# Inverse square roots of the layer norms: a power on GpSimd and one Newton step, instead of a bit trick and three steps on VectorE

## The chip, the core and the metric

The kernel runs on one core of one Trainium2 chip. The metric is the device time of one execution in microseconds (us). The profile names the engines: PE is TensorE's matrix products and PEld its weight loads, DVE is VectorE, ACT is ScalarE, POOL is GpSimd, and SP is SyncE, whose queue issues nearly all DMAs. All engines run on their own, each through its own list of instructions in order, and they wait for one another through semaphores.

## The reference, cut to what matters

One transformer block with adaptive layer norm, on x of 2 batches x 2048 rows x 256 columns:

```
mod = silu(c) @ wmod                      # six rows of 256 for each batch
sa, ca, ga, sb, cb, gb = six parts of mod # |ga|, |gb| raised to at least 0.25
norm(x) = (x - mean(x)) / sqrt(var(x) + 1e-5)      # over the 256 columns

h = norm(x) * (1 + ca) + sa
q, k, v  = projections of h               # 16 heads, keys of 16, values of 64
attn = softmax(q k^T / 4, axis = query)   # normalised over the queries
x = x + ga * (attn v) @ output_proj

h = norm(x) * (1 + cb) + sb
f(a, w) = fp4(a) @ fp4(w)^T               # blocks of 16, scale max/6, 8 levels and a sign
x = x + gb * f(silu(f(h, w_gate)) * f(h, w_up), w_down)     # 704 hidden columns
```

The change concerns the 1 / sqrt(var + 1e-5) in the two norms.

## The kernel before

The work is cut into chains, Python generators that yield one operation (or a group) at a time. A planner (`Order`, L111) picks greedily, by estimated costs, due times and free buffers, which chain goes on next, and so writes out by hand the order of every engine's instructions. The estimates of an operation are in `Queue.estimate` (L287). For a POOL operation on two tensors it takes 0.08 us and 0.0023 us an element (L321), and 0.2 us for a dependence from one engine to another (`CROSS`, L113). All operations are recorded through L273, so the profile tells groups apart by tile names and not by lines. The planner also holds POOL and some forms on DVE apart (`port`).

The attention runs over 2 batches, 16 heads in each and 16 blocks of 128 keys in each head: 512 steps. In a step (`scores` L1031, `step` L1091) PE forms the scores of 128 keys and 2048 queries (`ps`) in two halves. DVE copies each half out of PSUM, negated and scaled, with the running minimum (`e<-ps`, its longest kind of work). POOL merges the two minima (`mn`). ACT takes the exponential with the sum (`z`). DVE forms `rz` = 1/z, POOL scales the values with it (`vn`), and PE adds up the output (`o<-e,vn`) some steps later (LAG, 4.5). Five `e` buffers and three places for scores in PSUM bound how far the engines run ahead of each other.

Beside these steps lie, by their due times:

- the first norm (`norm` L835). Batch 0's four groups of 512 rows are at the very start, before there is any attention to lie beside; batch 1's four groups stand beside the last heads of batch 0. A group's statistics (`ln_stats` L574) are followed by `ln_apply` (L611, tile `xn`, on ACT or DVE as the planner chooses), PE transposes (`ht`), two copies with scale and bias (`ht`, one on ACT, one on DVE), and the q, k and v projections (`qk`, `v`). The copies `st` feed DMAs that bring q and k into the layout for the scores.
- the quantising of the weights (`quantize_exactly` L703, tiles `wg`, `wu`, `wd`, `qx`, `sp`), in batch 0.
- the output projections (`project` L1181, tiles `op`, `x`).
- the feed-forward part of batch 0 (`ffn_stats` L1266, `ffn` L1290), beside the attention of batch 1. It quantises its rows on DVE, ACT and POOL (`quantize` L648).
- after the last step, the tail: the last projections, the second norm (`ffn_stats`, `tail_norm` L1375) and the feed-forward part of batch 1 (`tail` L1404), with no attention left beside it.

At the start ACT also forms the modulation's columns (`sa_t` and `ca_t`, from PE's product `modt`); the modulation's rows (`modb`, `mods`) come from PE and are reworked on DVE. A filler of identity transposes (`busy`) runs on PE before that.

`ln_stats` (L574) is called with up to 4 tiles of 128 rows. For each it runs two statistics instructions (`bst` and `mv`, in the profile `sta`/`mva` or `stf`/`mvf`). Then it works on 128 x 4 values: `ln0` is the variance plus 1e-5, `ln1` the inverse root, `ln2` a scratch, `ln3` the mean times minus the root. Tiles of the first norm end in a, those of the second in f. The inverse root comes from shifting the bits of `ln0` right by one and subtracting them from a constant (L590 to L593), and then three Newton steps, of three operations each in the first two and four in the last (L594 to L600). All of it is on DVE. Each of these tiles has two buffers, and the room `ln` lets two calls be under way at once.

Of the kernel before, what the change touches and what calls it, by code (L numbers as in the profile page):

```python
# [10 lines left out]
F32 = mybir.dt.float32  # L11
F32R = mybir.dt.float32r
I32 = mybir.dt.int32
U32 = mybir.dt.uint32
AF = mybir.ActivationFunctionType
ALU = mybir.AluOpType
# [4 lines left out]
P = 128  # L21
# [313 lines left out]
def adaln_block(  # L335
# [14 lines left out]
    nc = tc.nc  # L350
# [24 lines left out]
    T, V, A, G, S = (  # L375
        Queue(n, e)
        for n, e in (
            ("PE", nc.tensor),
            ("DVE", nc.vector),
            ("ACT", nc.scalar),  # L380
            ("POOL", nc.gpsimd),
            ("SP", nc.sync),
        )
# [11 lines left out]
    const = ctx.enter_context(tc.tile_pool(name="const", bufs=1))  # L395
# [96 lines left out]
    ident = const.tile([P, P], F32, tag="ident", name="ident")  # L492
    make_identity(nc, ident)
    magic = const.tile([P, 2], F32, tag="magic", name="magic")
    nc.gpsimd.memset(magic[:, 0:1], 1.5 * 2.0 ** 22)
    nc.gpsimd.memset(magic[:, 1:2], -1.5 * 2.0 ** 22)

# [76 lines left out]
    def ln_stats(x4, name, centre=False):  # L574


        n = x4.shape[1]
        yield Wait(take=["ln"])
        mv = small.tile([P, 4, 2], F32, tag="mv", name=f"mv{name}", bufs=2)
        for t in range(n):  # L580
            st = small.tile([P, 6], F32, tag="bst", name=f"st{name}_{t}")
            yield Free(V.bn_stats(st, x4[:, t, :]))
            yield V.bn_aggr(mv[:, t, :], st)
        v, r, e, c = (
            small.tile([P, 4], F32, tag=f"ln{i}", name=f"ln{i}{name}", bufs=2)[:, 0:n]
            for i in range(4)
        )
        yield V.tensor_scalar(v, mv[:, 0:n, 1], EPS, None, ALU.add)

        yield V.tensor_scalar(r.bitcast(U32), v.bitcast(U32), 1, None, ALU.logical_shift_right)  # L590
        yield V.tensor_scalar(
            r.bitcast(I32), r.bitcast(I32), -1.0, float(0x5F3759DF), ALU.mult, ALU.add
        )  # L593
        for i in range(3):  # L594
            yield V.tensor_tensor(e, r, r, ALU.mult)
            yield V.scalar_tensor_tensor(e, e, -0.5, v, ALU.mult, ALU.mult)
            if i < 2:
                yield V.scalar_tensor_tensor(r, e, 1.5, r, ALU.add, ALU.mult)
        yield V.scalar_tensor_tensor(e, e, 0.5, r, ALU.add, ALU.mult)
        yield V.tensor_tensor(r, r, e, ALU.add)  # L600
        if centre:
            return mv[:, :, 0], r
        yield V.scalar_tensor_tensor(c, mv[:, 0:n, 0], -1.0, r, ALU.mult, ALU.mult)
        return c, r
# [230 lines left out]
    def norm(b, g):  # L835
# [8 lines left out]
        if b not in h_t:  # L844
            h_t[b] = hp.tile([P, KC, N], F32, tag="ht", name=f"ht{b}")
        c, r = yield from ln_stats(x4, f"a{b}_{g}")
        if b == 0:
            place, _ = yield Wait(["sa"], ["s", "e"])
# [417 lines left out]
    def ffn_stats(b, t, n):  # L1266
        yield Wait([("out", b, NQUAD - 1, t + j) for j in range(n)])
        x4 = xs[b, t // 4][:, t % 4 : t % 4 + n, :]
        c, r = yield from ln_stats(x4, f"f{b}_{t}", centre=b == B - 1)
        for j in range(n):  # L1270
            lns[b, t + j] = (c, r, j, n)
        signal(("ln", b, t))
# [361 lines left out]
```

## Time and profile before

| what | value |
|---|---|
| median of 3 runs | 1929.37 us (1929.2 to 1930.44) |
| the profiled execution's own time | 1929.38 us |
| its span, first to last instruction | 1927.6 us |
| granted TensorE clock | 1.00 |
| DVE, 128 x 4 `ln2a<-ln1a` product | 24 times, 152 ns each |
| POOL, 128 x 1 `mn<-mn` | 512 times, 298 ns each |
| POOL, 128 x 64 `vn<-v,rz` | 512 times, 323 ns each |
| first scores on PE (`ps<-q,k`) | at 42.38 us |
| last attention output on PE before the tail's first projection | until 1749.3 us |

A line of the timeline or of a group names the engine, the operation, the tile written and the tiles read (`out<-in`), and the shape. A timeline line begins with the start in us from the span's start and the duration; in brackets at its end is the idle time of the engine just before it, and what ended that. A group's line ends with the busy time, the mean of one in ns, and the idle time of the engine just before these instructions. The chain of waits is followed back from the last instruction: at each step to what released it, or to the instruction before it on its engine.

### The profile page before, as it was taken

How to read it: one execution, taken by the hardware profiler on the slowest of the kernel's cores; microseconds unless marked ns; L12 is line 12 of the kernel's file. 1: busy time of each engine (PE TensorE's matmuls, PEld its weight loads, DVE VectorE, ACT ScalarE, POOL GpSimd, SP SyncE). 2: the span in 40 equal slices, each digit the busy share in tenths (PEclk: the TensorE clock that was granted, in tenths of full speed). 3: DMA queues.
4: the chain of work that ended last, by engine and by line, in shares of the span. 5: the costliest groups of instructions: out<-in, count | busy, mean ns of one | idle time of the engine just before them, and what ended most of it. 6: DMA issues, size and time to landing. Idle time of an engine off the chain costs nothing.

```text
span 1927.6 us, 30282 instructions
## 1 busy us (share of the span) xinstructions
PE 1898.0 (98%) x10212; PEld 787.2 (41%) x10212; DVE 1711.0 (89%) x4170; ACT 1317.7 (68%) x1428; POOL 617.2 (32%) x1387
## 2 busy tenths in 40 slices
PE   9999999999999999999999999999999999999998
PEld 5333433343334333343334434334434343335666
DVE  5999999999999998888888788887888888997997
ACT  4787677777776676777777667676676777884333
POOL 0333333333443331113444344444443211230010
PEclk9999999999999999999999999999999999999999
DMA  6422121202120223211102210211011111100000
GB/s 211 100 67 55 38 56 50 47 19 49 46 62 4 50 55 94 77 39 45 52 16 61 64 44 18 55 36 39 9 37 44 34 34 34 39 1 1 12 17 17
DMA packets 40395, 88.02 MB, mean 46 GB/s; under 512 B 6320, under 2 KB 22576, under 8 KB 36272
## 3 DMA queue, kind: packets, MB, share of 16 engines
q1 hardware_dynamic: 38880, 83.98, 16.9%
q8 instruction: 82, 1.34, 0.3%
q10 hardware_dynamic: 1360, 2.10, 0.3%
q14 instruction: 73, 0.60, 0.1%
HBM read 63.51 MB, written 20.97 MB: 44 GB/s over the span
## 4 chain that ended last, share of the span: by engine, by line
PE 84%; DVE 13%; ACT 2%; issue 1%; POOL 0%; ACTq 0%; POOLq 0%; DVEq 0%
PE o L273 43%; PE ps L273 15%; DVE e L273 8%; PE op L273 6%; PE v L273 6%; PE dn L273 3%; PE qk L273 2%; PE up L273 2%; PE gate L273 2%; PE h2t L273 1%; DVE w L273 1%; PE pg L273 1%; PE pu L273 1%; ACT e L273 1%; PE busy L273 1%
## 5 line engine op out<-in xcount | busy, mean ns | idle before, releaser
L273 DVE TENSOR_SCALAR_CACHE_REDUCE e<-ps 128x1024 f32<-128x1024 f32 x1024 | 1226.1, 1215 | 90.5 <-PE ps L273 65.6
L273 ACT ACTIVATE e<-e,mn 128x2048 f32<-128x2048 f32 x512 | 1025.2, 2002 | 393.1 <-POOL mn L273 391.3
L273 PE MATMUL o<-e,vn 128*64 128x512 f32 x4096 | 993.4, 603 | 5.9 <-ACT osb L273 2.2
L273 PEld LDWEIGHTS o<-e,vn 128*64 128x64 f32 x4096 | 255.0, 136 | 454.1 <-issue 371.4
L273 POOL TENSOR_SCALAR mn<-mn 128x1 f32<-128x1 f32 x512 | 152.3, 298 | 731.4 <-DVE rz L273 285.3
L273 PE MATMUL ps<-q,k 64*128 64x512 f32 x2048 | 371.4, 445 | 2.2 <-DVE e L273 1.7
L273 PEld LDWEIGHTS ps<-q,k 64*128 64x128 f32 x2048 | 159.7, 184 | 346.6 <-DVE e L273 116.4
L273 POOL TENSOR_SCALAR vn<-v,rz 128x64 f32<-128x64 f32 x512 | 165.5, 323 | 309.2 <-DVE rz L273 217.4
L273 PE MATMUL op<-wo,osb 128*64 128x256 f32 (+1 forms) x960 | 125.3, 382 | 2.5 <-DVE x L273 1.8
L273 PE MATMUL v<-wv,ht 128*64 128x256 f32 x1024 | 124.0, 381 | 0.9 <-DVE st L273 0.6
L273 DVE RECIPROCAL rz<-z 128x1 f32<-128x1 f32 x512 | 80.3, 157 | 26.5 <-ACT e L273 25.5
L273 PEld LDWEIGHTS op<-wo,osb 128*64 128x64 f32 (+1 forms) x960 | 74.3, 140 | 61.1 <-issue 22.6
L273 PEld LDWEIGHTS v<-wv,ht 128*64 128x64 f32 x1024 | 71.3, 137 | 65.0 <-issue 26.9
L273 ACT ACTIVATION_READ_ACCUMULATOR e<-e,mn 128x1 f32 x512 | 95.4, 186 | 0.0
L273 DVE DVE_READ_ACCUMULATOR e<-ps 128x1 f32 x1024 | 84.2, 82 | 0.0
L273 ACT COPY osb<-o 64x512 f32<-64x512 f32 x104 | 60.2, 579 | 23.6 <-PE o L273 21.7
L273 PE MATMUL qk<-ht,wqk_sb 128*64 128x512 f32 (+1 forms) x224 | 61.7, 598 | 0.9 <-ACT ht L273 0.9
L273 POOL TENSOR_TENSOR h<-h,m 128x704 f32<-128x704 f32 x32 | 54.1, 1689 | 12.6 <-DVE m L273 7.9
L273 DVE TENSOR_TENSOR x<-op,x 128x512 f32<-128x512 f32 (+1 forms) x61 | 41.2, 676 | 13.7 <-PE op L273 13.3
L273 PE MATMUL dn<-wdb,e 117*128 117x256 f32 (+1 forms) x192 | 45.1, 382 | 3.3 <-ACT e L273 3.1
L273 ACT ACT_TABLE_LOAD x34 | 43.6, 1283 | 4.3 <-issue 3.7
L273 PE MATMUL dn<-wd_t,h2t 117*64 117x256 f32 (+1 forms) x384 | 45.8, 381 | 0.0
(243 smaller groups left out, 1454.8 us busy)
## 6 DMA issues: line engine op xcount, KB each, us to landing
k<-scr SPq DMA_DIRECT2D x124, 256.0 KB, 4.6
scr<-st SPq DMA_DIRECT2D x32, 512.0 KB, 3.2
q<-scr SPq DMA_DIRECT2D x124, 128.0 KB, 5.6
x<-in_x_dram SPq DMA_DIRECT2D x8, 512.0 KB, 4.4
wv<-in_wv_dram SPq DMA_DIRECT2D x8, 256.0 KB, 3.7
wo<-in_wo_dram SPq DMA_DIRECT2D x8, 256.0 KB, 2.7
xt<-in_x_dram SPq DMA_DIRECT2D x4, 512.0 KB, 7.2
out_dram<-h2t SPq DMA_DIRECT2D x16, 128.0 KB, 1.8
```

Of the source, the lines that this page charges most:

```text
L273: op = Op(self.name, *self.estimate(method, args, kw, lambda: f(*args, **kw)))
```

## The change

`ln_stats` takes the inverse root from one instruction on POOL, which raises `ln0` to the power of -0.5 (a tensor of exponents, `half_root`, is set once at the start), and keeps one Newton step of four operations on DVE. The bit trick and two Newton steps are gone. The planner's estimates are unchanged, so POOL's new instruction is planned as any product of two tensors of 4 elements.

```diff
     magic = const.tile([P, 2], F32, tag="magic", name="magic")
+    half_root = const.tile([P, 4], F32, tag="half_root", name="half_root")
+    nc.gpsimd.memset(half_root, -0.5)
     nc.gpsimd.memset(magic[:, 0:1], 1.5 * 2.0 ** 22)
...
         yield V.tensor_scalar(v, mv[:, 0:n, 1], EPS, None, ALU.add)
 
-        yield V.tensor_scalar(r.bitcast(U32), v.bitcast(U32), 1, None, ALU.logical_shift_right)
-        yield V.tensor_scalar(
-            r.bitcast(I32), r.bitcast(I32), -1.0, float(0x5F3759DF), ALU.mult, ALU.add
-        )
-        for i in range(3):
-            yield V.tensor_tensor(e, r, r, ALU.mult)
-            yield V.scalar_tensor_tensor(e, e, -0.5, v, ALU.mult, ALU.mult)
-            if i < 2:
-                yield V.scalar_tensor_tensor(r, e, 1.5, r, ALU.add, ALU.mult)
+        yield G.tensor_tensor(r, v, half_root[:, 0 : r.shape[1]], ALU.pow)
+        yield V.tensor_tensor(e, r, r, ALU.mult)
+        yield V.scalar_tensor_tensor(e, e, -0.5, v, ALU.mult, ALU.mult)
         yield V.scalar_tensor_tensor(e, e, 0.5, r, ALU.add, ALU.mult)
         yield V.tensor_tensor(r, r, e, ALU.add)
```

In the code `v`, `r` and `e` are the tiles `ln0`, `ln1` and `ln2`; `V` is DVE and `G` is POOL.

## The prediction

> **What bounds the kernel now.** I read the page's busy times and slices first, then the stretches (busy time of each engine in chosen windows), then the timeline of the first 45 us, and last the chain of waits of the tail.
>
> ```profile
> PE 1898.0 (98%) x10212; PEld 787.2 (41%) x10212; DVE 1711.0 (89%) x4170; ACT 1317.7 (68%) x1428; POOL 617.2 (32%) x1387
> ```
>
> TensorE (PE) idles 29.6 us of 1927.6. VectorE (DVE) has 89% and could bind where its share is higher. So I ask stage by stage.
>
> ```profile
> 15.00:42.40 27.40, 24.90 (x103) 11.56 (x101) 15.74 (x66) 14.35 (x25) 0.00 (x0) 1.00 0.60 175
> 640.00:720.00 80.00, 76.78 (x408) 27.93 (x405) 79.41 (x239) 57.27 (x62) 24.72 (x58) 1.00 0.16 40
> 900.00:1500.00 600.00, 598.99 (x3474) 240.89 (x3472) 506.80 (x1222) 420.53 (x445) 266.13 (x481) 1.00 0.16 40
> 1800.00:1880.00 80.00, 74.41 (x321) 54.14 (x320) 77.29 (x222) 28.11 (x47) 6.26 (x5) 1.00 0.04 15
> ```
>
> The columns are the stretch, its length, and PE, PEld, DVE, ACT and POOL busy with instruction counts. From 900 to 1500, where the feed-forward part of batch 0 lies beside attention, PE is full (598.99 of 600) and DVE has 15% to spare: there a shorter DVE stream buys nothing. From 640 to 720, where batch 1 is normalised, DVE is full (79.41 of 80) and PE is not. The tail is alike: the chain of waits from 1774 to 1880 runs mostly over DVE.
>
> ```profile
> by line: DVE e L273 32.3%; DVE w L273 17.1%; DVE am_g L273 8.0%; PE pg L273 6.9%; PE pu L273 5.9%; DVE r_g L273 3.7%; issue 3.1%; PE dn L273 2.7%; DVE am_h L273 2.6%; POOL w L273 2.3%; DVE q_g L273 1.9%; DVE stf L273 1.8%; ACT e L273 1.8%;
> ```
>
> At the start the timeline decides:
>
> ```profile
> 16.85 0.81 DVE L273 TENSOR_SCALAR ht<-ht,ca_t,sa_t 128x512 f32<-128x512 f32 x1 [3.59 <-ACT ht L273]
> ...
> 17.58 0.15 DVE L273 SCALAR_TENSOR_TENSOR ln1a<-ln2a,ln1a 128x4 f32<-128x4 f32 x1
> ...
> 19.19 0.14 DVE L273 SCALAR_TENSOR_TENSOR ln3a<-mva,ln1a 128x4 f32<-128x4 f32 x1
> ...
> 19.37 2.08 ACT L273 ACTIVATE xn<-x,ln3a,ln1a 128x256 f32<-128x256 f32 x4 [2.55 <-DVE ln3a L273]
> ...
> 27.38 2.07 ACT L273 ACTIVATE xn<-x,ln3a,ln1a 128x256 f32<-128x256 f32 x4 [1.38 <-DVE ln3a L273]
> ```
>
> The square-root chain of the second group of rows was cut in two: DVE sat 3.59 us at an ht copy with the rest of the chain queued behind, and ScalarE got its scale only at 19.37. The third group's came at 27.38. Both waits are on the serial path to the first scores at 42.38.
>
> **The change part by part.** ln_stats is called 17 times (ln1 is shifted 8 times for the attention norms and 9 times for the feed-forward norms). Each call loses 8 DVE instructions (2 of the bit trick, 2 x 3 of two Newton steps) and gains one on POOL: 136 off DVE, 17 onto POOL and one memset. The built order agrees: DVE has 136 rows fewer, POOL 18 more, counting that memset.
>
> *Price of a removed step.* Its row says 152 ns, but steps overlap when their neighbours are independent. Taken as the distance from its start to the next DVE start, one costs 114 ns in the first 60 us, 84 ns around 640 to 720, 161 ns in batch 0's feed-forward part and 96 ns in the tail. Times 32, 32, 32 and 40: 3.6, 2.7, 5.2 and 3.8 us of DVE.
>
> *Price of the power.* No row shows one.
>
> ```profile
> L273 POOL TENSOR_SCALAR mn<-mn 128x1 f32<-128x1 f32 x512 | 152.3, 298 | 731.4 <-DVE rz L273 285.3 <-DVE e L273 280.2 <-ACT e L273 41.0
> L273 POOL TENSOR_TENSOR h<-h,m 128x704 f32<-128x704 f32 x32 | 54.1, 1689 | 12.6 <-DVE m L273 7.9 <-DVE rz L273 4.0 <-ACT m L273 0.3
> ```
>
> Below, it is POOL's smallest form, 0.30 us; above, I take POOL's longest row, 1.69 us. With 4 elements it is nearest to the first, and I take p = 0.4 us, an estimate; both ends stay in the range. Nothing makes it a gain below zero: POOL has never done this step.
>
> *The waits that it adds.* POOL waits for ln0 from DVE; behind it stand the softmax's mn and vn. DVE then waits for the power at its first product, and everything on DVE stands behind that. In the built order the DVE work between ln0 and that product is: start, a copy and two statistics (0.75 us); one instruction; 1.5 us of copies and a statistic; nothing. Batch 1's norms: one softmax reduction (1.2 us), in the last group two. Batch 0's feed-forward: one reduction, then nothing three times. Tail: nothing; 1.1 us; 1.5 us; several us twice.
>
> *Start.* ScalarE's first xn waits in order behind sa_t, which PE's modt releases at 13.26, so the first power is free up to about 1.7 us. The second group's product may start at 12 us and has until the ht copy at 16.85: hidden up to about 3.5. In the new order only ln3a is left behind that copy, so xn starts at about 17.8 instead of 19.37, and one of its four parts goes to DVE. Third group: seven statistics and sums bring ln0 to about 20.5, the st copy and the ht copy follow to 22.4 (power hidden up to 1.9), then about 1.5 us of remaining chain among statistics: xn at 24.0 instead of 27.38. Fourth group: xn at about 28.8 instead of 31.71, ht complete at 32.1 instead of 37.1. Behind that stand one q projection (1.72), two modb products (0.86 each) and one v (1.87), so the first scores come at about 37.7, 4.7 us sooner. But the new order puts the second v product (1.87) and one modb (0.86) behind them, and from 42.4 on PE is full (56.96 of 57.6): 2.7 us come back. Net **-2.0**. The extra memset (98 ns, 0.03 apart from its neighbour) stands ahead of the identity that PE waits for at 1.37: under 0.1, in the rounding.
>
> *Batch 1's norms.* DVE is full, so 2.7 us count, less 0.5 for the 15 us or so of these 80 in which PE is full as well: **-2.2**. The 1.2 us reduction covers p = 0.4 and two crossings (mn ends at 45.72 and ScalarE's exponential starts at 45.75, so under 0.1 each). Without that cover it would cost 4 x 0.5.
>
> *Feed-forward of batch 0.* PE covers all of it; nothing won, and a DVE stall of 0.5 us is lost in its 15% of idle time: **0**.
>
> *Tail.* 24 of 40 steps (2.3 us) lie in the stretch from 1768 on where DVE is the path; 16 (1.5 us) lie before, among projections that keep PE nearly full, of which I count half. Less one bare wait of 0.5 us: **-2.5**. What is late next there is DVE's quantising, so the rest follows.
>
> Sum: -2.0 - 2.2 - 2.5 = -6.7, and 0.3 back for the mn and vn that now stand behind a power. The profiled execution took 1929.38 (span 1927.6 and 1.78 around it), the median of the runs is 1929.37; so **1923.0**.
>
> At p = 1.69 the batch 1 norms lose 3 x 0.6 and the tail about 2, so about 1927: the upper end of this case.
>
> **The rivals.**
> *The power takes microseconds* (slower). An instruction that works out a power in software may take many passes. Beyond their covers DVE stands still in turn: three norms of batch 1 lose p - 1.05 each, the tail p + 0.1, p - 1.1 and p - 1.5, the start p - 1.7 and p - 1.9. At p = 2.0 that is about 6.7, all that is won: the point from which it decides. Ten passes at the smallest row (0.30) would be 3.0 us: start +2.9, norms +6.6, tail +6.5, some 16 in all, 1938.5. For it: no arithmetic row of POOL is a power, and the planner still prices it as 4 plain elements, so it gave it no room. Against it: 4 elements are very little, and the longest row is under 2.0.
>
> *PE covers it all.* The steps around 640 and in the tail are off the path, since PE has 93 to 96% there, and another greedy order loses as much as it wins. Only the start's 2.0 counts: 1927.4. For it: the whole order after the first group is new. Against it: PE changes between row, column and full tiling about as often (1028 before, 1024 now), and the same number of other instructions stands on DVE.
>
> *Its first use is slow.* A first power at about 10 us that took 6 us longer would hold up the first xn, free up to 1.7 us: +4.4, 1927.4. Against it, POOL's first tensor product at 71.16 took 0.62, the mean of its group (0.622), and the first mn 0.29.
>
> The rule behind this rival is in the Trainium skill, GPSIMD Engine Reference, section 2.1: the first call of a freshly loaded kernel on that engine pays about 6 us (5.95 measured) for its code. The trace shows no such pause at POOL's first uses, so by it the sum would be 1927.4 only if the power were not resident.
>
> That the change does not do what it says is excluded by the counts above.
>
> **How the numbers follow.** Forecast 1923.0, faster: 0.50; its own range is 1918 to 1927. PE covers it: 0.15. Slow first use: 0.07. Microseconds: 0.28. A measurement of this kernel can tell about 0.2% (3.9 us) from no change, so the second and third are "same". Faster 0.50, same 0.22, slower 0.28. The range runs from 1918 (all 3.8 of the tail and 2.7 of the norms count, 1 us of luck in the order) to 1939 (p = 3); beyond it I leave about 0.15, longer powers above all.
>
> **What would show it.** The rows of ln1<-ln0,half_root on POOL give p at once; under 1.7 the forecast's steps stand. First scores near 38 instead of 42.38 and xn of the third group near 24 show the start. DVE busy should fall by about 15 us to 1696, with PE's idle time at 640 to 720 down from 3.2 to about 1. A "DVE ln2 <- POOL ln1" wait of more than 1 us a time would show the slow rival; it, a first power much longer than the others, or DVE still full after 640 with PE no denser would make the prediction wrong.

## The result, and the profile after

The changed kernel takes **1923.93 us** (median of 7 runs, 1923.44 to 1924.69), the kernel before 1929.37 (median of the 7 runs beside it, 1929.13 to 1930.6). The ratio is 0.997, 95% interval 0.9961 to 0.998: 5.4 us less, where the forecast was 1923.0. The profiled execution took 1924.16, with a span of 1922.4. The total is right; three of the steps that make it up are not.

The page of the changed kernel, its span and busy times:

```profile
span 1922.4 us, 30166 instructions
...
PE 1895.5 (99%) x10212; PEld 786.1 (41%) x10212; DVE 1698.2 (88%) x4033; ACT 1318.4 (69%) x1426; POOL 640.7 (33%) x1406
```

DVE is 12.8 us less busy and POOL 23.5 more, the 17 powers being 18.6 of that. DVE has 137 instructions fewer and POOL 19 more. They stand in these groups (form and count, then busy time and mean in ns, then the idle time ahead of them and what ended it):

```profile
L273 POOL TENSOR_TENSOR ln1f<-ln0f,half_root 128x4 f32<-128x4 f32 x7 | 8.9, 1274 | 34.4 <-DVE ln0f L273 34.3
L273 POOL TENSOR_TENSOR ln1a<-ln0a,half_root 128x4 f32<-128x4 f32 x8 | 8.2, 1031 | 21.8 <-DVE ln0a L273 19.7 <-DVE ln3a L273 1.2 <-DVE sh_wd L273 0.8
L273 POOL TENSOR_TENSOR ln1f<-ln0f,half_root 128x3 f32<-128x3 f32 x1 | 0.9, 862 | 4.6 <-DVE ln0f L273 4.6
L273 POOL TENSOR_TENSOR ln1f<-ln0f,half_root 128x1 f32<-128x1 f32 x1 | 0.6, 584 | 7.1 <-DVE ln0f L273 7.1
```

So p is 1.03 us and not 0.4 (the mean of 1.27 is due to one power of 2.53 at 1843.8; the others of four elements lie between 1.007 and 1.116). From one to four elements a partition it grows by 0.15 us each, over 0.43.

The timeline of the start, down to the first scores:

```profile
9.97 1.06 POOL L273 TENSOR_TENSOR ln1a<-ln0a,half_root 128x4 f32<-128x4 f32 x1 [8.61 <-DVE ln0a L273]
...
13.31 0.16 DVE L273 TENSOR_TENSOR ln2a<-ln1a 128x4 f32<-128x4 f32 x1 [1.07 <-POOL ln1a L273]
...
16.14 0.81 DVE L273 TENSOR_SCALAR ht<-ht,ca_t,sa_t 128x512 f32<-128x512 f32 x1 [1.72 <-ACT ht L273]
...
17.05 1.58 ACT L273 ACTIVATE xn<-x,ln3a,ln1a 128x256 f32<-128x256 f32 x3 [0.95 <-DVE ln3a L273]
...
22.48 2.08 ACT L273 ACTIVATE xn<-x,ln3a,ln1a 128x256 f32<-128x256 f32 x4 [2.53 <-DVE ln3a L273]
...
27.20 1.09 ACT L273 ACTIVATE xn<-x,ln3a,ln1a 128x256 f32<-128x256 f32 x2 [0.67 <-DVE ln3a L273]
...
38.75 0.73 PE L273 MATMUL ps<-q,k 64*128 64x512 f32 x4
```

The start moved much as forecast: `xn` of the second, third and fourth group at 17.05, 22.48 and 27.20 (forecast 17.8, 24.0, 28.8; before 19.37 and 27.38 for the second and third), and the first scores at 38.75 instead of 42.38 (forecast 37.7). The stretches of the norms of batch 1 and of the tail:

```profile
640.00:720.00 80.00, 77.81 (x406) 27.73 (x406) 76.87 (x206) 61.51 (x69) 28.45 (x62) 1.00 0.18 45
1800.00:1880.00 80.00, 75.53 (x323) 54.94 (x322) 75.08 (x205) 27.43 (x45) 11.34 (x8) 1.00 0.04 15
```

In the first, DVE (third sum) is no longer full, and PE idles 2.2 us instead of 3.2. In the second, DVE fell from 77.29 to 75.08 and PE rose from 74.41 to 75.53. The chain of waits from 1774 to 1880 now reads:

```profile
by line: PE pg L273 21.1%; PE dn L273 16.8%; PE pu L273 15.6%; DVE e L273 13.1%; DVE w L273 8.5%; PE h2t L273 4.4%; ACT e L273 3.2%; ACT w L273 2.7%; DVE am_g L273 2.5%; DVE am_h L273 2.0%; DVE r_g L273 1.7%; DVE s_g L273 1.6%; issue 1.2%; 
```

Its largest entries were DVE's; they are PE's feed-forward products now. DVE's waits for the power:

```profile
DVE ln2f L273 <- POOL ln1f L273: 4.9, 6, 1.3
...
DVE ln2a L273 <- POOL ln1a L273: 2.8, 3, 1.2
```

Of the 4.9 us, 4.0 are the four calls of batch 0's feed-forward and 0.9 the tail; the 2.8 are all in the start, and there is no wait in the norms of batch 1. There the power lies under the reduction that stands between `ln0` and the product:

```profile
644.88 1.22 DVE L273 TENSOR_SCALAR_CACHE_REDUCE e<-ps 128x1024 f32<-128x1024 f32 x1
...
645.12 1.03 POOL L273 TENSOR_TENSOR ln1a<-ln0a,half_root 128x4 f32<-128x4 f32 x1
...
646.18 0.16 DVE L273 TENSOR_TENSOR ln2a<-ln1a 128x4 f32<-128x4 f32 x1
```

**Where the time went.** The 512 exponentials on ACT count the attention steps, so the time at which the k-th begins compares two executions at the same progress. The columns give what each profiled execution gains (negative) or loses on the kernel before, in us, from the start to step 192 (before batch 1's norms), to step 256 (after them), to step 512 (batch 0's feed-forward lies in between), and to the end. Between these marks PE has the same number of products in every run (but for one, in e8).

| run | start | batch 1's norms | attention with feed-forward 0 | tail | median of the runs |
|---|---|---|---|---|---|
| changed kernel | -0.62 | -2.56 | +1.11 | -3.15 | 1923.93 |
| e1 power in the start alone | -0.12 | 0.00 | +0.09 | -0.03 | 1929.19 |
| e2 in batch 1's norms alone | -0.34 | -2.52 | +0.14 | -0.01 | 1926.81 |
| e3 in batch 0's feed-forward alone | +1.53 | +0.01 | +1.30 | -0.01 | 1930.52 |
| e4 in the tail alone | -0.07 | +0.01 | +0.05 | -2.93 | 1926.21 |
| e5 power twice, planned | +2.65 | +1.90 | +3.51 | -0.20 | 1937.24 |
| e6 one step on DVE, no power | -0.69 | +8.29 | -0.12 | -1.75 | 1935.52 |
| e7 all but feed-forward 0 | -0.33 | -2.54 | +0.12 | -2.86 | 1923.39 |
| e8 planner told the price | +2.97 | -2.71 | +0.11 | -1.08 | 1928.37 |
| e9 as e6, old norms of batch 1 | +0.17 | -0.01 | -0.13 | -0.14 | 1926.95 |
| e10 as e7, without the Newton step | +3.45 | +5.36 | -0.01 | -2.20 | 1935.98 |
| e11 norms of batch 1 and tail | -0.19 | -2.53 | +0.22 | -3.13 | 1923.75 |
| e12 power twice, same order | +2.16 | +0.75 | +5.29 | -0.06 | 1937.42 |

The start's column holds up to a microsecond that no edit makes: the filler's 64th transpose begins at 11.27 before and at 9.92 to 11.25 in the other executions (below). In the changed kernel it comes 0.71 sooner. So it does in e2, whose start is that of the kernel before and whose column shows -0.34; of the changed kernel's -0.62 some 0.3 is left.

**What else changed places.** The planner wrote the whole order anew, and with it moved work between engines. Between steps 192 and 256, in the changed kernel and in each run that gains 2.5 us there, three `ht` copies, four `osb` copies and one `xn` went from DVE to ACT: 5.5 us by their rows, where the 32 removed steps have 4.9. DVE's copies there, two lines before and two after:

```profile
L273 DVE TENSOR_SCALAR ht<-ht,ca_t,sa_t 128x512 f32<-128x512 f32 x6 | 4.7, 805 | 0.3 <-ACT ht L273 0.3
L273 DVE COPY osb<-o 64x512 f32<-64x512 f32 x5 | 3.4, 685 | 1.1 <-ACT osb L273 1.0
```

```profile
L273 DVE TENSOR_SCALAR ht<-ht,ca_t,sa_t 128x512 f32<-128x512 f32 x3 | 2.4, 807 | 0.7 <-PE ht L273 0.4 <-ACT ht L273 0.3
L273 DVE COPY osb<-o 64x512 f32<-64x512 f32 x1 | 0.7, 683 | 0.0
```

In the tail some 2.0 us of the quantising's products went from DVE to POOL (POOL's, before and after):

```profile
L273 POOL TENSOR_TENSOR e<-e,s_g 128x704 f32<-128x704 f32 x3 | 4.2, 1387 | 41.8 <-DVE q_h L273 18.7 <-DVE am_g L273 16.1 <-DVE am_h L273 7.0
```

```profile
L273 POOL TENSOR_TENSOR e<-e,s_g 128x704 f32<-128x704 f32 x5 | 6.9, 1387 | 39.1 <-DVE am_h L273 14.5 <-ACT e L273 10.4 <-DVE q_h L273 9.2
```

In the start and in batch 0's feed-forward copies went the other way, some 2.4 us onto DVE in each. No run takes the steps off DVE without such moves, or makes the moves alone.

### The profile page after: what moved, and what is told of

It reads as the page before. It is cut to its first block, busy times and chain, and to the rows that moved or that the text cites. A ratio compares the mean times of both kernels' runs of the same rounds, so it can differ in the third digit from the quotient of the medians.

```text
span 1922.4 us, 30166 instructions
## 1 busy us (share of the span) xinstructions
PE 1895.5 (99%) x10212; PEld 786.1 (41%) x10212; DVE 1698.2 (88%) x4033; ACT 1318.4 (69%) x1426; POOL 640.7 (33%) x1406
## 5 line engine op out<-in xcount | busy, mean ns | idle before, releaser
L273 DVE TENSOR_SCALAR_CACHE_REDUCE e<-ps 128x1024 f32<-128x1024 f32 x1024 | 1226.7, 1215 | 92.2 <-PE ps L273 72.5
L273 DVE TENSOR_TENSOR x<-op,x 128x512 f32<-128x512 f32 (+1 forms) x61 | 41.2, 675 | 13.5 <-PE op L273 13.1
```

Of the source, the lines that this page charges most:

```text
L273: op = Op(self.name, *self.estimate(method, args, kw, lambda: f(*args, **kw)))
```

## The experiments

**One place at a time: e1 to e4.** Each uses the power for the calls of one place, by the name of the call ("a0" in e1, "a1" in e2, "f0" in e3, "f1" in e4), and the bit trick and three steps elsewhere. Against the changed kernel, with the lines of the bit trick left out:

```diff
...
+        power = name.startswith("a0")
+        if power:
+            yield G.tensor_tensor(r, v, half_root[:, 0 : r.shape[1]], ALU.pow)
+        else:
...
+        for i in range(2 if power else 0, 3):
```

e1, expected: 

> The power replaces the bit trick and two Newton steps only in batch 0's four first norms, at the start; all other norms keep the old chain. Theory (time is won where VectorE's stream is the path): at equal TensorE work the changed kernel was 0.6 us ahead from 195 us on, so about 1928.7, with the first exponential near 42.2 instead of 45.7. Rival (the whole gain is the start, the rest only shifts work about): about 1924. Rival (re-planning): anything from 1927 to 1931, with a lead that comes and goes in stages the edit does not touch.

Measured: 1929.19 (1928.24 to 1929.48), ratio 0.9997 (0.9988 to 1.0005). The start alone shows no gain, though the first exponential begins at 42.68 instead of 45.75.

e2, expected: 

> The power only in batch 1's four first norms, which lie beside the last heads of batch 0. Theory: VectorE is full there and loses 2.7 us of work, the 1.03 us of a power lie under a softmax reduction; the lead at 320 steps after them grew by 1.2 to 2.5 us in the changed kernel: 1927.0 to 1928.2. Rival (TensorE covers it): 1929.4. Rival (re-planning): no relation to the removed work, 1927 to 1931.

Measured: 1926.81 (1926.64 to 1928.25), ratio 0.9987 (0.9978 to 0.9996), 2.5 us less.

e3, expected: 

> The power only in the four norms ahead of batch 0's feed-forward part, where TensorE is full. Theory: nothing is won and a wait of 1 us on VectorE is lost in its idle time: 1929.4, within 0.7. Rival (re-planning alone moves the time by microseconds): off by 1 us or more to either side, since everything behind the first of these norms is planned anew.

Measured: 1930.52 (1930.27 to 1932.21), ratio 1.0007 (0.9998 to 1.0016): 1.25 us more, though the interval reaches 1. The profile supports a loss: +1.30 between steps 256 and 512, and DVE waits there 4.0 us over the four calls. The +1.53 in its start is the granted clock, below.

e4, expected: 

> The power only in the five norm calls of the tail. Theory: the tail of the changed kernel was 3.1 us shorter, with VectorE on the path: 1926.2, and the last exponential where it was before, 1743.8. Rival (the tail is shorter because the stages before left it another order): 1929.4. The four parts should add up to the whole: start 0.6, norms 1.2 to 2.5, feed-forward 0, tail 3.1, together 5 to 6 us of 5.4 measured; if they do not add up within 1.5, re-planning has a share.

Measured: 1926.21 (1925.94 to 1926.47), ratio 0.9982 (0.9973 to 0.9991), 3.1 us less. The four parts sum to -0.1 - 2.5 + 1.25 - 3.1 = -4.4, beside -5.4 for the whole.

**The price of the power with the planner in between: e5.**

```diff
+        yield G.tensor_tensor(e, v, half_root[:, 0 : r.shape[1]], ALU.pow)
         yield G.tensor_tensor(r, v, half_root[:, 0 : r.shape[1]], ALU.pow)
```

Expected: 

> A second power of the same size stands ahead of the real one on GpSimd (its result is overwritten), so that the power and its double take some 2.06 us where the one took 1.03. Theory of the prediction's slow rival (what the power takes beyond the DVE work between ln0 and the product is paid by DVE): batch 1's norms lose 3 x 1.0, the tail 1.0 + 1.0 + 0.6, the start 0.5 at most, about +5.6 to +6.1 against the changed kernel, 1929.5 to 1930, so that the whole gain is gone. Rival (the power's wait is covered by PE or by other DVE work in most places, and only bare waits count, one in the tail): +1 to +2, 1925 to 1926. A second rival, that the planned order decides and not the wait: within 1.5 of the changed kernel either way, with no longer wait of DVE for ln1.

Measured: 1937.24 (1935.85 to 1937.57), ratio 1.0038 (1.0025 to 1.005): 13.3 us above the changed kernel, twice what the first theory allowed. But the planner counted the second power, and the order of the whole kernel moved; the granted clock of the profiled execution also fell, to 0.65 at 24 to 28 us and 0.63 at 700 to 704. So the price is not read from it but from e12, at the end.

**The same number of DVE instructions and two, without a wait: e6.**

```diff
-        for i in range(3):
-            yield V.tensor_tensor(e, r, r, ALU.mult)
-            yield V.scalar_tensor_tensor(e, e, -0.5, v, ALU.mult, ALU.mult)
-            if i < 2:
-                yield V.scalar_tensor_tensor(r, e, 1.5, r, ALU.add, ALU.mult)
+        yield V.tensor_tensor(e, r, r, ALU.mult)
+        yield V.scalar_tensor_tensor(e, e, -0.5, v, ALU.mult, ALU.mult)
```

(against the kernel before; the bit trick and the last two operations stay.)

Expected: 

> No power: the bit trick and the last Newton step alone, all on DVE. Two of the three Newton steps are left out, so that the root is good to about two parts in a thousand only; the number of instructions on DVE is that of the changed kernel and two more in each of the 17 calls. It shows what the power and its crossing cost beside two steps of DVE. If the power's wait costs DVE what its row says (1.0 us less the cover in the batch 1 norms, 1.1 and more in the tail, 4 us over four calls in batch 0's feed-forward), this is 2 to 3 us faster than the changed kernel, 1921 to 1922, and the 1.25 us that batch 0's feed-forward lost is back. If the waits are covered and the loss there is one of the planned order, it is 1923 to 1925, since two DVE steps more cost some 1 us in norms and tail.

Measured: 1935.52 (1934.62 to 1936.15), ratio 1.0031 (1.0019 to 1.0042). Neither theory holds: 10.9 us are lost on the changed kernel in the norms of batch 1. The timeline of DVE in the last of these norms shows how it begins:

```profile
688.77 0.43 DVE L273 BATCH_NORM_STATS2 sta<-xt 128x6 f32<-128x256 f32 x1 [2.72 <-DMA xt<-in_x_dram]
```

and the stretches from 688 on, the granted clock being the last column but two:

```profile
688.00:692.00 4.00, 1.32 (x8) 0.47 (x4) 3.23 (x10) 1.16 (x2) 0.23 (x1) 0.85 0.02 5
692.00:696.00 4.00, 4.00 (x12) 1.06 (x10) 2.87 (x11) 2.23 (x3) 0.35 (x2) 0.50 0.00 0
696.00:700.00 4.00, 4.00 (x17) 1.37 (x16) 4.00 (x11) 2.35 (x3) 0.78 (x2) 0.80 0.00 0
```

In the new order the next group's statistics stand ahead of the landing of their rows (whose DMA is issued at 682.71 here, at 683.01 in the changed kernel, where DVE does not wait for it). DVE stands 2.72 us, PE works 1.32 of 4 us, and then it runs at half its clock. PE idles 2.7 us at this place, and the low clock costs some 2.8 by the last two rows (half of 4 us and a fifth of 4). Between steps 192 and 256, over the same 1120 products, PE idles 9.28 us here and 2.86 in the changed kernel, and is busy 215.38 and 210.95: 6.4 of the 10.9 us are idle time and 4.4 longer products. No single wait explains what is left. So this run tells nothing of the power in that stage, only that the stage can lose ten microseconds by its order. Outside it, it says two things, repeated by e9.

**Without that stage: e9.** As e6, with all three steps in the calls named "a1".

```diff
-        for i in range(3):
+        for i in range(2 if not name.startswith("a1") else 0, 3):
```

Expected: 

> No power: the bit trick and one Newton step on DVE in the start, in batch 0's feed-forward and in the tail, all three steps in the norms of batch 1 (two Newton steps are left out in 13 of the 17 calls, so that those roots are good to two parts in a thousand). It takes out of the run before it the place where that one lost 10 us, DVE's 2.72 us wait for the rows xt of the last norm, and shows the three other places without any wait for GpSimd. If the loss in batch 0's feed-forward is the wait for the power, the lead stays level there (no loss between steps 271 and 447), and with 1.7 from the tail the time is 1927 to 1927.8. If that loss comes from any other order of the feed-forward's work, 1 us or more is lost there too: 1928.3 to 1929. If the 10 us did not come from that wait, they are here as well: 1935 and more.

Measured: 1926.95 (1926.71 to 1929.64), ratio 0.999 (0.9981 to 0.9999), as the first theory said. Batch 0's feed-forward stays level (-0.13): 24 DVE steps fewer win nothing there, and without a wait for POOL nothing is lost. That speaks for the wait as the cause of e3's loss. It doesn't prove it, since the planner also spread the feed-forward's copies otherwise here than in e3; e12 tries the wait with the order held. The tail is at -1.75 in e6. This run's PE starts in the tail, counted from step 512, agree with those of e6 to 0.01 us until the last stretch; there, in the profiled execution (1929.26, one of the two slowest of the eleven), the clock fell to 0.84 at 1912 to 1916 and 0.74 at 1916 to 1920, and 1.6 us were lost again.

**The wait taken out: e7.** Power in all calls except those named "f0"; the edit is that of e1 to e4 with

```diff
+        power = not name.startswith("f0")
```

Expected: 

> Power everywhere except in batch 0's feed-forward norms, which keep the bit trick and three steps. If the loss of 1.25 us that the power alone showed there adds to the rest: 1922.7, about 1.2 under the changed kernel. If that loss was one of the planned order and not of the power: 1923.9, or anywhere within 1.5 of it.

Measured: 1923.39 (1923.1 to 1924.16), ratio 0.9969 (0.9957 to 0.998). The stage is level again (+0.12 instead of +1.11). The medians differ by 0.54 only, half of the forecast 1.2 and within the spread of the runs; it is the lowest time of the study, not shown to be lower than the changed kernel's.

**The planner told: e8.**

```diff
+            if ALU.pow in args:
+                return 0.42 + 0.155 * n, emit
             if n == 1:
```

Expected: 

> The changed kernel with the planner told what the power takes (0.42 + 0.155 us for each element, 1.04 us for four, where it counted 0.09). If the planner can put other DVE work between ln0 and the product, the DVE waits for ln1 (4.9 us over 6 in the feed-forward norms, 2.8 over 3 in the attention norms) shrink to under half, and the time falls by 1 to 2 us to 1922 to 1923. Rival: there is no ready work to put there, or the greedy order loses as much elsewhere: the waits stay and the time is within 1 us of 1923.9.

Measured: 1928.37 (1928.18 to 1928.66), ratio 0.9994 (0.9985 to 1.0003). DVE's waits for `ln1` did fall, from 7.7 us over nine times to 2.8 over four. The feed-forward's loss is gone, though two waits of 0.4 and 1.1 us stand there still; but 3.6 us (0.7 of it the filler's) are lost in the start and 2.1 in the tail, counted from the changed kernel. PE idles there in the first 60 us 6.62 instead of 4.55. The right price made the waits shorter and the kernel 4.4 us slower than the changed one: what the greedy order moved cost more than the waits it took out.

**Fewer DVE steps still: e10.** As e7, without the four operations of the last step (the root is then the power itself).

```diff
-        yield G.tensor_tensor(r, v, half_root[:, 0 : r.shape[1]], ALU.pow)
-        yield V.tensor_tensor(e, r, r, ALU.mult)
-        yield V.scalar_tensor_tensor(e, e, -0.5, v, ALU.mult, ALU.mult)
-        yield V.scalar_tensor_tensor(e, e, 0.5, r, ALU.add, ALU.mult)
-        yield V.tensor_tensor(r, r, e, ALU.add)
+        if not name.startswith("f0"):
+            yield G.tensor_tensor(r, v, half_root[:, 0 : r.shape[1]], ALU.pow)
+        else:
...
```

(Behind `else` stand the bit trick and the three steps.)

Expected: 

> The power alone, without the last Newton step, in the start, the norms of batch 1 and the tail; batch 0's feed-forward keeps the bit trick and three steps. The root is then as exact as the power itself. 52 DVE instructions fewer than with power and one step outside the feed-forward part. Theory (DVE sets the time in norms and tail, at 84 and 96 ns a step): 16 x 84 + 20 x 96 ns = 3.3 us, of which the norms and the tail gave back two thirds to four fifths so far: 1920.5 to 1921.5. Rival (with fewer instructions between, the power's crossing stands bare in a row with the next operation, or the faster chain meets the landing of xt in the last norm as the run without a power did): no gain, 1923 to 1924, or 1930 and more if DVE waits for xt.

Measured: 1935.98 (1935.34 to 1936.51), ratio 1.0034 (1.0022 to 1.0047). Both theories miss: DVE doesn't wait for xt here, and still the start loses 3.45 and the norms 5.36, with PE idle for 6.58 us in the first 60 (before: 4.52) and 6.71 from 620 to 800. Even the tail, where DVE's steps count, gained less (-2.20) than with the step kept (-2.86). In the start the granted clock fell to 0.65 at 28 to 32 us, and three `v` copies went from DVE to ACT, as in e5 and e8, which lose 2.65 and 2.97 there; in the changed kernel three went the other way. What exactly the new order does wrong was not tried.

**The start left out: e11.** Power in the calls named "a1" and "f1" alone.

```diff
+        power = name.startswith(("a1", "f1"))
```

Expected: 

> Power in the norms of batch 1 and in the tail alone; start and batch 0's feed-forward keep the bit trick and three steps. If the parts add (2.46 and 3.06 from the runs of one part each): 1923.8. If the start is worth something after all, this is slower than the version with power everywhere but in batch 0's feed-forward (1923.4) by that: the forecast's 2.0 would make it 1925.4.

Measured: 1923.75 (1923.61 to 1924.89), ratio 0.9972 (0.9962 to 0.9983). The parts add. e7, which has the power in the start too, is 0.36 lower by its median, within the spread: that is all that the start shows.

**The price of the power alone: e12.** The planner emits each power twice and counts it once; the order of the instructions on the five engines is that of the changed kernel, with 17 powers more.

```diff
+            if ALU.pow in args:
+                once, emit = emit, lambda: (once(), once())[1]
             if n == 1:
```

Expected: 

> Every power is issued twice in a row into the same tile, with the planned order of all engines as in the changed kernel (the planner does not count the second one, whereas in the earlier doubling it did, and the whole order moved). So p goes from 1.03 to about 2.05 us and nothing else changes: the price of the power itself. By the prices of the prediction's slow rival: batch 1's norms 3 x 1.0, the tail 1.0 + 1.0 + 0.6, the start up to 0.5, and by the run of batch 0's feed-forward alone another 1 us there: +5.6 to +7.1 on the changed kernel, 1929.5 to 1931. If most of the 13.3 us of the earlier doubling was the power's own: 1935 and more, with the granted clock down in the start or in the last norms as there. If the covers hold in this order (DVE has other work ahead of most products): +1 to +3, 1925 to 1927.

Measured: 1937.42 (1934.83 to 1937.93), ratio 1.0038 (1.0024 to 1.0051). This is the clean measure: 1.02 us more for each power cost 13.5 us. Against the changed kernel the stages lose 2.78, 3.31, 4.18 and 3.09. The waits show why. DVE at the four norms of batch 1, where the changed kernel has none (the last of the four is still covered):

```profile
650.07 0.16 DVE L273 TENSOR_TENSOR ln2a<-ln1a 128x4 f32<-128x4 f32 x1 [1.17 <-POOL ln1a L273]
...
673.03 0.16 DVE L273 TENSOR_TENSOR ln2a<-ln1a 128x4 f32<-128x4 f32 x1 [1.02 <-POOL ln1a L273]
...
695.05 0.16 DVE L273 TENSOR_TENSOR ln2a<-ln1a 128x4 f32<-128x4 f32 x1 [1.11 <-POOL ln1a L273]
...
713.57 0.14 DVE L273 TENSOR_TENSOR ln2a<-ln1a 128x4 f32<-128x4 f32 x1
```

Three bare waits, 3.3 us in sum, cost 3.3 us. In batch 0's feed-forward the second call waits 1.16 us in the changed kernel and 2.24 here:

```profile
1006.69 0.16 DVE L273 TENSOR_TENSOR ln2f<-ln1f 128x4 f32<-128x4 f32 x1 [1.16 <-POOL ln1f L273]
```

```profile
1015.25 0.16 DVE L273 TENSOR_TENSOR ln2f<-ln1f 128x4 f32<-128x4 f32 x1 [2.24 <-POOL ln1f L273]
```

The four waits there grow by 4.6 us and the stage by 4.2. The clock adds to it in two places: in the start, 0.84 at 24 to 28 and 0.73 at 28 to 32, after PE had idled 2.16 us for `xn`, and in the tail, 0.61 at 1860 to 1864, after 2.25 us for `w`. One of the five executions, with a mean clock of 1.000, took 1934.83, and the four at 0.998 took 1937.17 to 1937.93; so some 2.6 us go with the clock, in both places together, and 10.9 are left for the power.

## Why the prediction was right, step by step

The theory was that DVE's shorter chains count where DVE sets the time and that a short power hides; the main rival that the power's wait takes it all back. The total held, 1923.93 for 1923.0, but in part by luck. The terms were -2.0 for the start, -2.2 for the norms, 0 for batch 0's feed-forward and -2.5 for the tail, with 0.3 back; the stages of the profiled executions show -0.62, -2.56, +1.11 and -3.15. What was missing in the first and third came partly back in the others.

- **The price of a removed step, and what of it counts: near in size, the cause shown in part.** Norms of batch 1: forecast -2.2, measured -2.5 (e2, e11). Tail: forecast -2.5, measured -3.1 (e4). That DVE's time counts in the norms is shown by e12, where 3.3 us of waits in a held order cost 3.3. But the sum took the removed steps as all that changes on DVE, and they are not. Between steps 192 and 256 DVE is busy for 196.1 us before and 189.6 after, the copies that went to ACT being about half of that, and only 1.4 of PE's 2.6 us are idle time less; its same 1120 products took 1.1 less. For the tail, e6 takes out 30 of the 40 steps and moves 1.1 us of products instead of 2.0, and gains 1.75. So how much of either term is the steps' own stays open. The prediction had counted 136 rows off DVE and 18 onto POOL and concluded that the same other work stands on DVE; the trace has 137 and 19, and stage by stage up to eight instructions changed engines.
- **p = 0.4: wrong.** "With 4 elements it is nearest to the first" took the smallest POOL row as the nearest; measured 1.03, within the two ends given. The total stood because the covers were rightly read: the norms' cover of 1.2 us hides 1.03 (no wait in the changed kernel, three of 1.0 to 1.2 us in e12). Break-even was put at 2.0; by e12 some 5.4 us are lost over 0.4 to 0.5 us more, so it lies, in a straight line through the two kernels, near 1.45, or 1.55 without the clock's share; that is a rough estimate, since a cover hides a wait up to its own length and nothing beyond. The margin above 1.03 was 0.4 to 0.5 us, half of what the prediction would have given it.
- **The start's -2.0: wrong.** The events came as worked out, but "net -2.0" took the 4.7 us of earlier scores less 2.7 of postponed products for a gain. PE's own total says otherwise. In the first 60 us PE was busy, first before, then after:

```profile
0.00:60.00 60.00, 55.48 (x284) 32.38 (x286) 38.68 (x147) 29.78 (x46) 3.68 (x17) 1.00 0.61 184
```

```profile
0.00:60.00 60.00, 55.45 (x292) 32.16 (x294) 37.68 (x113) 29.09 (x44) 8.28 (x22) 1.00 0.60 184
```

  The same, to 0.03 us. The scores came sooner because the projections and rows of the modulation came later, and the idle time only moved (PE idles 1.42 us for `xn` of the third group, until 23.13, and 0.69 for a copy of the output, until 104.95, which it did not before). e1 and e11 show no gain from the start that is clear of their spread.
- **Feed-forward of batch 0, 0: wrong by its wait.** That the removed steps win nothing is right (e9). "A DVE stall of 0.5 us is lost in its 15% of idle time" is not: the four waits, 4.0 us in sum (0.4, 1.2, 1.3 and 1.2), go with a loss of 0.5 (the changed kernel against e7) to 1.25 (e3), and 4.6 us more of them, in a held order, with 4.2 (e12). DVE's idle time is in good part of another kind: over the whole changed kernel 72.5 us of it stand ahead of its reductions of scores, waiting for PE. The likely reason, which no run tries by itself, is that it can't be spent at another moment, while a wait for the power holds up the next reduction, and PE soon after: of the 950 us from 800 to 1750 PE is busy for 948.42 before, 947.47 in the changed kernel and 944.79 in e12.
- **0.3 for `mn` and `vn`:** nothing in the runs separates it.
- **The rivals.** *Microseconds of power*: not this p, but the mechanism is real. From p = 1.03 to 2.05 its prices give 3.0 for the norms, 2.5 for the tail and 0.5 for the start, measured (e12) 3.3, 3.1 and 2.8, the last two with the clock's 2.6; the 4.2 in the feed-forward part were missing. For p = 3.0 the same prices give 2.4 for the start and 5.9 for the norms, not the 2.9 and 6.6 that were added up. *PE covers it all*: fell by the time, since the norms and the tail gained; its doubt about the greedy order was right, as the moves above and e6, e8 and e10 show. *A slow first use*: fell. The first power took 1.057 us, the next ones 1.007 to 1.044; the 6 us that the Trainium skill, GPSIMD Engine Reference, section 2.1, gives for the first call of a freshly loaded kernel do not appear in front of this instruction.
- **What would show it.** DVE's busy time was to fall by 15 to 1696; it fell by 12.8 to 1698.2. PE's idle time from 640 to 720 was to fall to about 1 and fell to 2.2. What is late next in the tail was to be DVE's quantising; PE's products lead the chain.

What stays open: why two kernels with slightly other chains on DVE (two operations more a call than the changed kernel in e6, four fewer in e10) lose 8 to 11 us on it around batch 1's norms. For e6 the landing of `xt` and the clock are shown, for half of it at most. In both, PE idles some 5 us behind step 220, 1.7 of it at once before `v` products that wait for DVE (at 808.59 in e6, at 809.81 in e10), where the changed kernel has no idle time. And of the `ht`, `osb` and `xn` copies DVE keeps 15 in e6 and 17 in e10 (17 before), but 9 in the five kernels that gain 2.5 us there (the changed one, e2, e7, e8, e11). That gain is no more than one good order of this stage against bad ones that are near.

## What to carry to other kernels

Where an operation moves to another engine, price the wait by what the waiting engine has between the operand and the first use, place by place. An average of idle time need not cover a bare wait in front of work that feeds the full engine. Before a gain is put down to the operations that were removed, count stage by stage what else changed engines. An event that comes sooner at the start is no gain before the busy time of the full engine over the whole stretch says so. And where a planner writes the order, measure a cost with the order held still (as in e12), or its shuffling of up to 10 us is taken for the cost.

## What the runs showed of the hardware

- POOL's power takes 0.58, 0.86 and 1.03 us for 1, 3 and 4 elements a partition, where its plain operation on one element (`mn`) takes 0.30. One of four elements took 2.53 us, in the tail, with DVE busy beside it on 512 and 704 columns a partition; the first of the pair at that place in e12 took 2.535. In e5 and e10, where the tail's last power stands beside other work, it took 1.007. What lengthens it was not tried.
- PE's clock halves after short idle times, and not in each execution of the same order. e3 and the kernel before run the same instructions up to 60 us with the same idle times of 0.93 and 1.17; in e3's profiled execution the clock then fell, and a q or k projection of four products took 2.95 us instead of 1.88:

```profile
22.00:26.00 4.00, 4.00 (x8) 1.70 (x7) 3.59 (x17) 0.93 (x2) 0.00 (x0) 0.57 0.49 140
```

  Three of its eleven runs lie at 1931.7 to 1932.2, the others at 1930.3 to 1930.6. The Trainium skill, TensorE: Matmul & The Clock Gate, section "What's actually happening", gives a half-speed state after an idle window of about 3.4 us that runs free of the kernel. The rows agree on the half (0.50 at 692 to 696 in e6) and on the chance, but the idle times here are parts of such a window, 1 to 3 us, with work in between.
- The filler's transposes go from 0.214 to 0.109 us each at a moment that differs between executions, with the granted clock at 1.00 throughout. The 64th begins up to 1.35 us sooner by it. In e6 and e9, whose order is the same up to step 192, it begins 0.94 apart, and step 192 comes 0.86 apart.
